# A row-by-row product kernel: four batch rows per instruction, and four 14.6 KB packets where one of 57 KB was stored

## The chip, the cores and the metric

The kernel runs on one core of a Trainium2 chip. The metric is the device time of one execution in microseconds (us). Medians are quoted. In the views of the profile VectorE is DVE, ScalarE is ACT and SyncE, which issues the stores, is SP. A packet, in the profile, is a run of bytes that one of the core's 16 DMA engines moves in one piece; in the stores it is one contiguous run of a partition (before: 9,600 such packets of 4,096 to 58,624 B for 75 stores of 128 partitions).

## The reference

For each of 4,096 batch rows of 256 fp32 numbers, the output holds all products x[i]·x[j] with j ≥ i, one triangle row after the other:

```python
def _L0_rec_ref(inputs):                     # inputs: [4096, 256] float32
    d = inputs.shape[1]
    dot = jnp.einsum('bi,bj->bij', inputs, inputs)
    iu, ju = jnp.triu_indices(d)
    return dot[:, iu, ju]                    # [4096, 32896] float32
```

The input is 4.2 MB and the output 539 MB. The work is one multiplication per number stored.

## The kernel before

A group is 512 batch rows: 128 partitions with four batch rows each. A partition's four output rows lie one behind the other in memory, so they are treated as one run of 131,584 numbers and cut into nine pieces of about 14,600. Each piece has one buffer, filled by multiplications of a single triangle row (`tensor_scalar` on VectorE or `activation` on ScalarE, shared out by estimated time), and is stored by one DMA in which each partition is one contiguous run of 57 KB.

```python
x_in = x.rearrange("(g p r) d -> p g r d", p=P, r=REPEAT)        # REPEAT = 4
x_out = out.rearrange("(g p r) c -> g p (r c)", p=P, r=REPEAT)
xt = xpool.tile([P, groups, REPEAT, d], F32, name="x")
...                                                              # loads cut
for g in range(groups):
    for c, (lo, hi) in enumerate(zip(borders, borders[1:])):     # nine pieces
        o = opool.tile([P, slot], F32, tag="o", name=f"o_{g}_{c}")   # three buffers
        cuts = [lo, *FIRST, hi] if g == c == 0 else [lo, hi]
        for a, b in zip(cuts, cuts[1:]):
            shares.even()
            for row, i, j, at, length in runs(d, a, b):
                shares.multiply(o[:, at - lo : at - lo + length],
                                xt[:, g, row, j : j + length],
                                xt[:, g, row, i : i + 1], length)
            nc.sync.dma_start(x_out[g][:, a:b], o[:, a - lo : b - lo])
```

Of the kernel before, what the change touches and what calls it, by code (L numbers as in the profile page):

```python
# [1 line left out]

# [4 lines left out]

F32 = mybir.dt.float32
AF = mybir.ActivationFunctionType
ALU = mybir.AluOpType  # L10

P = 128
UNIT = 64


def even_borders(lo: int, hi: int, pieces: int) -> list[int]:
    units = (hi - lo) // UNIT
    return [lo + units * c // pieces * UNIT for c in range(pieces)] + [hi]


def runs(d: int, lo: int, hi: int):


    width = d * (d + 1) // 2
    for row in range(lo // width, (hi + width - 1) // width):
        at = row * width
        for i in range(d):
            a, b = max(at, lo), min(at + d - i, hi)
            if a < b:
                yield row, i, i + a - at, a, b - a  # L30
            at += d - i


class Shares:


    def __init__(self, nc):
        self.nc = nc
        self.vector = self.scalar = 0.0

    def even(self):
        self.vector = self.scalar = 0.0

    def multiply(self, dst, src, factor, length: int):
        v = self.vector + 130 + 0.51 * length
        s = self.scalar + 187 + 0.83 * length
        if v <= s:
            self.vector = v
            self.nc.vector.tensor_scalar(dst, src, factor, None, ALU.mult)  # L49
        else:  # L50
            self.scalar = s
            self.nc.scalar.activation(dst, src, AF.Copy, scale=factor)  # L52


REPEAT = 4
PIECES = 9
FIRST = [1024, 3072, 7168]


@with_exitstack  # L60
def kernel(
    ctx: ExitStack, tc: tile.TileContext, x: bass.AP, out: bass.AP
):




    nc = tc.nc
    n, d = x.shape
    width = out.shape[1]  # L70
    assert n % (P * REPEAT) == 0 and width == d * (d + 1) // 2
    groups = n // (P * REPEAT)
    total = REPEAT * width
    assert total % UNIT == 0
    borders = even_borders(0, total, PIECES)
    slot = max(b - a for a, b in zip(borders, borders[1:]))

    xpool = ctx.enter_context(tc.tile_pool(name="x", bufs=1))
    opool = ctx.enter_context(tc.tile_pool(name="o", bufs=3))

    x_in = x.rearrange("(g p r) d -> p g r d", p=P, r=REPEAT)
    x_out = out.rearrange("(g p r) c -> g p (r c)", p=P, r=REPEAT)

    xt = xpool.tile([P, groups, REPEAT, d], F32, name="x")
    cuts = sorted({0, 1, groups // 8, groups // 2, groups})
    for a, b in zip(cuts, cuts[1:]):
        if a < b:
            nc.sync.dma_start(xt[:, a:b], x_in[:, a:b])

    shares = Shares(nc)  # L90
    for g in range(groups):
        for c, (lo, hi) in enumerate(zip(borders, borders[1:])):
            o = opool.tile([P, slot], F32, tag="o", name=f"o_{g}_{c}")
            cuts = [lo, *FIRST, hi] if g == c == 0 else [lo, hi]
            for a, b in zip(cuts, cuts[1:]):
                shares.even()
                for row, i, j, at, length in runs(d, a, b):
                    shares.multiply(
                        o[:, at - lo : at - lo + length],
                        xt[:, g, row, j : j + length],  # L100
                        xt[:, g, row, i : i + 1],
                        length,
                    )
                nc.sync.dma_start(x_out[g][:, a:b], o[:, a - lo : b - lo])  # L104


# [1 line left out]
_INS = ["r_inputs"]  # L108
_OUTS = [((4096, 32896), "float32")]


# [20 lines left out]
```

## Time and profile before

| | before |
|---|---|
| time, median of 3 (range) | 1287.72 us (1287.57 to 1287.92) |
| VectorE busy | 977 us, 4,961 instructions |
| ScalarE busy | 968 us, 3,299 instructions |
| data moved, packets of the data queue | 543.17 MB, 11,872 |
| packets of the instruction queue | 66 |

The first lines to read are the data queue's share (98.0%) and what ended the engines' idle time (stores): both are quoted in the prediction below, with the last windows of the span. One more line completes the picture. It is the chain of work that ended last, followed back from the end and summed by line.

```profile
DMA out_dram<-o 65%; DVE o L49 31%; DMA x<-in_r_inputs_dram 0%; DVEq L49 0%; SPq L104 0%; DVEq L128 0%
```

Two thirds of the chain is storing; VectorE's third are the steps by which a freed buffer is filled again. A buffer comes free when the latest engine is done with it: the last four stores land 0.4 to 0.5 us after every eighth packet of the engine that ends at 1284.6 us, and VectorE goes on 0.12 to 0.13 us after a landing.

### The profile page before, as it was taken

What the parts mean: (1) busy time and instruction counts of PE and PEld (TensorE: products, weight loads), DVE (VectorE), ACT (ScalarE), POOL (GpSimd) and SP (SyncE); (2) the same over time, 40 slices, a digit from 0 to 9 for tenths busy, and PEclk for the clock granted to TensorE, in tenths of its full rate; (3) what the DMA queues carried; (4) which work ended last, traced back from release to release, by engine and by line L of the source; (5) the groups of instructions that cost most, each with busy time, mean ns of one, the idle gap of its engine ahead of it and who ended that gap; (6) DMA issues with size and microseconds to landing.
All of it is one profiled execution on the core that took longest, in us unless ns stands there. A gap on an engine that the chain in (4) does not pass through costs nothing.

```text
span 1285.9 us, 8601 instructions
## 1 busy us (share of the span) xinstructions
DVE 977.2 (76%) x4961; ACT 968.2 (75%) x3299; POOL 0.2 (0%) x4
## 2 busy tenths in 40 slices
DVE  8987778777777777777777777777777777688760
ACT  9987778777777777777777777777777777687760
POOL 0000000000000000000000000000000000000000
DMA  9999999999999999999999999999999999999995
GB/s 392 435 434 435 437 435 427 426 428 437 433 435 436 437 435 433 437 432 428 421 435 437 419 426 435 420 426 412 437 410 437 434 411 412 437 433 435 413 408 222
DMA packets 11938, 543.71 MB, mean 423 GB/s; under 512 B 1248, under 2 KB 1248, under 8 KB 2400
## 3 DMA queue, kind: packets, MB, share of 16 engines
q1 hardware_dynamic: 11872, 543.17, 98.0%
q14 instruction: 66, 0.54, 0.1%
HBM read 4.19 MB, written 538.97 MB: 422 GB/s over the span
## 4 chain that ended last, share of the span: by engine, by line
DMA 66%; DVE 31%; issue 0%; DVEq 0%; SPq 0%
DMA out_dram<-o 65%; DVE o L49 31%; DMA x<-in_r_inputs_dram 0%; DVEq L49 0%; SPq L104 0%; DVEq L128 0%
## 5 line engine op out<-in xcount | busy, mean ns | idle before, releaser
L49 DVE TENSOR_SCALAR o<-x 128x256 f32<-128x256 f32 (+53 forms) x4961 | 977.2, 288 | 274.1 <-DMA out_dram<-o 269.8
L52 ACT ACTIVATE o<-x 128x255 f32<-128x255 f32 (+62 forms) x3298 | 967.0, 387 | 282.2 <-DMA out_dram<-o 280.0
L52 ACT ACT_TABLE_LOAD x1 | 1.3, 1283 | 0.7 <-PEq L119 0.7
L119 POOL MEMSET const-bfloat16-1.0<- 128x1 bf16 x1 | 0.1, 101 | 0.0
L119 POOL MEMSET const-uint8-127<- 128x1 uint8 x1 | 0.1, 101 | 0.0
L119 POOL MEMSET const-float32-0.0<- 128x1 f32 x1 | 0.1, 98 | 0.2 <-issue 0.2
L119 POOL MEMSET const-float32-1.0<- 128x1 f32 x1 | 0.1, 98 | 0.0
## 6 DMA issues: line engine op xcount, KB each, us to landing
out_dram<-o SPq DMA_DIRECT2D x39, 7296.0 KB, 41.9
out_dram<-o SPq DMA_DIRECT2D x32, 7328.0 KB, 35.9
out_dram<-o SPq DMA_DIRECT2D x1, 3712.0 KB, 17.9
x<-in_r_inputs_dram SPq DMA_DIRECT2D x1, 2048.0 KB, 12.5
out_dram<-o SPq DMA_DIRECT2D x1, 2048.0 KB, 14.3
x<-in_r_inputs_dram SPq DMA_DIRECT2D x1, 1536.0 KB, 7.0
out_dram<-o SPq DMA_DIRECT2D x1, 1024.0 KB, 12.1
x<-in_r_inputs_dram SPq DMA_DIRECT2D x1, 512.0 KB, 3.3
```

What stands on the lines that cost most here:

```text
L49: self.nc.vector.tensor_scalar(dst, src, factor, None, ALU.mult)
L52: self.nc.scalar.activation(dst, src, AF.Copy, scale=factor)
L119: nc = _bacc.Bacc("TRN2", target_bir_lowering=False, num_devices=1)
```

## The change

One `tensor_tensor` multiplies the same triangle row, or two neighbouring ones, of all four batch rows. VectorE can do that with access patterns that step from batch row to batch row and repeat the factor (971 such instructions in the changed kernel). ScalarE gets only what VectorE has no time for. The store keeps its number of bytes, but in a buffer [partition, batch row, piece] a partition's share is four runs of 14.6 KB, which go to four output rows. The intent: far fewer instructions, at the price of more and shorter packets.

```diff
-    xt = xpool.tile([P, groups, REPEAT, d], F32, name="x")
+    total = n // P * d
+    xt = xpool.tile([P, total + 1], F32, name="x")      # a product of two rows reads one column more
+    nc.vector.memset(xt[:, total:], 0.0)
...                                                      # rows dealt out anew: "(p g r) c -> g p r c"
-            o = opool.tile([P, slot], F32, tag="o", name=f"o_{g}_{c}")
+            o = opool.tile([P, REPEAT, slot], F32, tag="o", name=f"o_{g}_{c}")
...                                                      # ScalarE's rows, vector_ops, split: cut
+                for way, (i, j, at, length) in interleave(block[k:]):
+                    if way == "each": ...               # four tensor_scalar, as before
+                    m = 2 if way == "two" else 1
+                    nc.vector.tensor_tensor(
+                        o[:, :, at : at + m * length].rearrange("p r (m l) -> p r m l", m=m),
+                        window(xt[:, row + j :], [[d, REPEAT], [1, m], [1, length]]),
+                        window(xt[:, row + i :], [[d, REPEAT], [1, m], [0, length]]),
+                        ALU.mult,
+                    )
-                nc.sync.dma_start(x_out[g][:, a:b], o[:, a - lo : b - lo])
+                nc.sync.dma_start(x_out[g][:, :, a:b], o[:, :, a - lo : b - lo])
```

More of the change, by code (lines that the diff above doesn't have):

```diff
@@ L13 @@
 UNIT = 64
+REPEAT = 4
+PIECES = 9
+BUDGET = 1.08
+FIRST = [512, 1536, 3584]
 def even_borders(lo: int, hi: int, pieces: int) -> list[int]:
@@ L18, in even_borders @@
     return [lo + units * c // pieces * UNIT for c in range(pieces)] + [hi]
-def runs(d: int, lo: int, hi: int):
-    width = d * (d + 1) // 2
-    for row in range(lo // width, (hi + width - 1) // width):
-        at = row * width
-        for i in range(d):
-            a, b = max(at, lo), min(at + d - i, hi)
-            if a < b:
-                yield row, i, i + a - at, a, b - a
-            at += d - i
-class Shares:
-    def __init__(self, nc):
-        self.nc = nc
-        self.vector = self.scalar = 0.0
-    def even(self):
-        self.vector = self.scalar = 0.0
-    def multiply(self, dst, src, factor, length: int):
-        v = self.vector + 130 + 0.51 * length
-        s = self.scalar + 187 + 0.83 * length
-        if v <= s:
-            self.vector = v
-            self.nc.vector.tensor_scalar(dst, src, factor, None, ALU.mult)
-        else:
-            self.scalar = s
-            self.nc.scalar.activation(dst, src, AF.Copy, scale=factor)
@@ L55, with runs, vector_ops @@
-REPEAT = 4
-PIECES = 9
-FIRST = [1024, 3072, 7168]
+def runs(d: int, lo: int, hi: int) -> list:
+    found, at = [], 0
+    for i in range(d):
+        a, b = max(at, lo), min(at + d - i, hi)
+        if a < b:
+            found.append((i, i + a - at, a, b - a))
+        at += d - i
+    return found
+def vector_ops(block: list) -> list:
+    ops, k = [], 0
+    while k < len(block):
+        i, j, at, n = block[k]
+        two = k + 2 < len(block) and i == j
+        each = REPEAT * (130 + 0.52 * n)
+        together = 68 + 1.046 * REPEAT * n - (34 if two else 0)
+        if each <= together:
+            ops.append(("each", block[k]))
+        elif two:
+            ops.append(("two", block[k]))
+            k += 1
+        else:
+            ops.append(("all", block[k]))
+        k += 1
+    return ops
@@ new lines, in interleave, with vector_time @@
+def interleave(block: list) -> list:
+    half, at = 0, sum(n for *_, n in block) / 2
+    while half < len(block) and at > 0:
+        at -= block[half][3]
+        half += 1
+    a, b = vector_ops(block[:half]), vector_ops(block[half:])
+    return [op for k in range(max(len(a), len(b))) for ops in (a, b) for op in ops[k : k + 1]]
+def vector_time(block: list) -> float:
+    t = 0.0
+    for way, (i, j, at, n) in vector_ops(block):
+        if way == "each":
+            t += REPEAT * (130 + 0.52 * n)
+        else:
+            t += 68 + 1.046 * REPEAT * n * (2 if way == "two" else 1)
+    return t
@@ L60, with split, window @@
+def split(block: list, budget: float) -> int:
+    scalar, k = 0.0, 0
+    while k < len(block):
+        scalar += REPEAT * (184 + 0.837 * block[k][3])
+        if vector_time(block[k:]) <= budget or scalar > vector_time(block[k + 1 :]):
+            break
+        k += 1
+    return k
+def window(ap: bass.AP, free: list) -> bass.AP:
+    return bass.AP(ap.tensor, ap.offset, [list(ap.ap[0]), *free])
 @with_exitstack
@@ L70 @@
     width = out.shape[1]
-    assert n % (P * REPEAT) == 0 and width == d * (d + 1) // 2
+    assert n % (P * REPEAT) == 0 and width == d * (d + 1) // 2 and width % UNIT == 0
     groups = n // (P * REPEAT)
-    total = REPEAT * width
-    assert total % UNIT == 0
-    borders = even_borders(0, total, PIECES)
+    borders = even_borders(0, width, PIECES)
     slot = max(b - a for a, b in zip(borders, borders[1:]))
@@ L79 @@
     opool = ctx.enter_context(tc.tile_pool(name="o", bufs=3))
-    x_in = x.rearrange("(g p r) d -> p g r d", p=P, r=REPEAT)
-    x_out = out.rearrange("(g p r) c -> g p (r c)", p=P, r=REPEAT)
-    xt = xpool.tile([P, groups, REPEAT, d], F32, name="x")
-    cuts = sorted({0, 1, groups // 8, groups // 2, groups})
+    x_in = x.rearrange("(p r) d -> p (r d)", p=P)
+    x_out = out.rearrange("(p g r) c -> g p r c", p=P, r=REPEAT)
+    total = n // P * d
+    xt = xpool.tile([P, total + 1], F32, name="x")
@@ L86 @@
+    nc.vector.memset(xt[:, total:], 0.0)
+    cuts = [0, REPEAT * d, total // 2, total]
     for a, b in zip(cuts, cuts[1:]):
-        if a < b:
-            nc.sync.dma_start(xt[:, a:b], x_in[:, a:b])
-    shares = Shares(nc)
+        nc.sync.dma_start(xt[:, a:b], x_in[:, a:b])
     for g in range(groups):
         for c, (lo, hi) in enumerate(zip(borders, borders[1:])):
-            o = opool.tile([P, slot], F32, tag="o", name=f"o_{g}_{c}")
-            cuts = [lo, *FIRST, hi] if g == c == 0 else [lo, hi]
+            o = opool.tile([P, REPEAT, slot], F32, tag="o", name=f"o_{g}_{c}")
+            first = g == c == 0
+            cuts = [lo, *(FIRST if first else []), hi]
@@ L95 @@
             for a, b in zip(cuts, cuts[1:]):
-                shares.even()
-                for row, i, j, at, length in runs(d, a, b):
-                    shares.multiply(
-                        o[:, at - lo : at - lo + length],
-                        xt[:, g, row, j : j + length],
-                        xt[:, g, row, i : i + 1],
-                        length,
+                block = runs(d, a, b)
+                k = split(block, 0.0 if first else BUDGET * REPEAT * (b - a))
+                for i, j, at, length in block[:k]:
+                    for r in range(REPEAT):
+                        row = (g * REPEAT + r) * d
+                        nc.scalar.activation(
+                            o[:, r, at - lo : at - lo + length],
+                            xt[:, row + j : row + j + length],
+                            AF.Copy,
+                            scale=xt[:, row + i : row + i + 1],
+                        )
@@ new lines @@
+                row = g * REPEAT * d
+                for way, (i, j, at, length) in interleave(block[k:]):
+                    at -= lo
+                    if way == "each":
+                        for r in range(REPEAT):
+                            row_r = row + r * d
+                            nc.vector.tensor_scalar(
+                                o[:, r, at : at + length],
+                                xt[:, row_r + j : row_r + j + length],
+                                xt[:, row_r + i : row_r + i + 1],
+                                None,
+                                ALU.mult,
+                            )
+                        continue
+                    m = 2 if way == "two" else 1
[3 more added lines that the diff above has]
+                        window(xt[:, row + i :], [[d, REPEAT], [1, m], [0, length]]),
+                        ALU.mult,
```

## The prediction

> **What bounds the kernel now.** I read the page first: the DMA queues beside the engines' busy shares, then the groups of instructions.
>
> ```profile
> DVE 977.2 (76%) x4961; ACT 968.2 (75%) x3299; POOL 0.2 (0%) x4
> ...
> q1 hardware_dynamic: 11872, 543.17, 98.0%
> q14 instruction: 66, 0.54, 0.1%
> HBM read 4.19 MB, written 538.97 MB: 422 GB/s over the span
> ...
> L49 DVE TENSOR_SCALAR o<-x 128x256 f32<-128x256 f32 (+53 forms) x4961 | 977.2, 288 | 274.1 <-DMA out_dram<-o 269.8
> L52 ACT ACTIVATE o<-x 128x255 f32<-128x255 f32 (+62 forms) x3298 | 967.0, 387 | 282.2 <-DMA out_dram<-o 280.0
> ```
>
> Both engines idle a fifth of the time, and nearly all of that waiting for a stored buffer to come free. The data queue is busy 98.0% of 16 DMA engines' span. So the store is the limit, and faster arithmetic alone buys nothing. What matters is the 2% that is not busy, and who has it. For that I cut the end of the span, after the last compute instruction, into windows of 2 us (columns: window and its length; DVE, ACT and POOL busy; clock; share of 16 DMA engines; GB/s, each packet counted where it starts).
>
> ```profile
> 1264.00:1266.00 2.00, 0.00 (x0) 0.00 (x0) 0.00 (x0) 1.00 1.08 469
> 1266.00:1268.00 2.00, 0.00 (x0) 0.00 (x0) 0.00 (x0) 1.00 1.08 469
> 1268.00:1270.00 2.00, 0.00 (x0) 0.00 (x0) 0.00 (x0) 1.00 0.14 59
> 1270.00:1272.00 2.00, 0.00 (x0) 0.00 (x0) 0.00 (x0) 1.00 0.14 59
> 1272.00:1274.00 2.00, 0.00 (x0) 0.00 (x0) 0.00 (x0) 1.00 0.14 59
> 1274.00:1276.00 2.00, 0.00 (x0) 0.00 (x0) 0.00 (x0) 1.00 0.07 29
> 1276.00:1278.00 2.00, 0.00 (x0) 0.00 (x0) 0.00 (x0) 1.00 0.00 0
> 1278.00:1280.00 2.00, 0.00 (x0) 0.00 (x0) 0.00 (x0) 1.00 0.07 29
> ```
>
> A packet here is one partition's 58,624 B, which in 2 us is 29 GB/s. Until 1268 all 16 engines start a packet per window (469 = 16 x 29). Then 14 of them have finished, two go on, and from 1274 one alone. The end of the kernel is one DMA engine that is 15 us late.
>
> Stringing the trace's single DMA packets (start, duration, size, queue) into 16 lines shows why. Packets follow each other without a gap. Fourteen lines end at 1269.6 us, one at 1275.5, one at 1284.6. From 739 us on each of the fourteen also stood idle for about 12 us in 8 gaps of 1.1 to 2.1 us, when no finished buffer was there, since buffers come free only when the latest engine is done. Without those they would have ended at about 1257.5, so the last engine has **27 us of extra work**. On the two late lines stand instruction-fetch packets of 8,192 B (309 ns), and the data packet beside such a fetch takes about 2.60 us on one of them and 2.35 us on the other instead of 2.15. The program has 5,040 VectorE and 3,378 ScalarE instructions; at 128 per packet that is 39 and 26 fetches. I infer that the last engine carries VectorE's: 27.1 us / 39 = 0.69 us each (309 + 450 ns by the single packets).
>
> [...] The old pitch is 526,336 B; the new is 4,210,688 B, that is 4 MiB + 16 KiB. [...]
>
> **The change, part by part.**
>
> 1. *Fewer instructions.* The built program has 1,892 on VectorE (848 tensor_scalar, 971 tensor_tensor, the rest mostly waits) and 633 on ScalarE. VectorE's fetches shrink in proportion: 27.1 x 1,892 / 5,040 = 10.2 us. On the line that sets the end: **-16.9 us**.
>
> 2. *Shorter packets.* Bytes stay. From start to start the trace's packets take 155.3 ns (4,096 B), 305.8 (8,192), 607 (16,384) and 2,150.6 (58,368): 0.03677 ns per byte plus 4.6 ns. A partition's piece is now four packets, three more. An engine has 8 partitions and 72 pieces: 576 x 3 x 4.6 ns = **+7.9 us**, on every line.
>
> 3. *Start.* The first piece must come from slower arithmetic. With about 130 + 0.52n ns per tensor_scalar (VectorE ran without a stop over the first 174: 34.99 us, 201 ns each at a mean length near 140, so it fits), piece 0 is ready at 4.0 + 11.4 = 15.4 us and piece 1 at about 30.9, near 32 with the issue. The queue has input until about 13 us and then 17.8 us of piece 0, until about 31. **+1 us** of an idle queue on all lines.
>
> 4. *VectorE.* [...] A group of nine pieces then has some 120 tensor_tensor over 98,920 elements, 111 us, and 108 tensor_scalar, 28 us: 139 us against 9 x 17.4 = 157 us of storing. But the built program makes 102 instructions of a group wait for the one directly before them, although the code interleaves two halves to avoid that: a two-row product is taken to overlap everything between its first and last element. Completion trails the next start by 357 - 263 = 94 ns at 256 columns, and from VectorE's last end to the store's issue 60 ns pass, so such a wait should cost some 150 ns: 15 us more, 154 of 157. It stays just hidden. The first two-row product of a piece likewise waits for ScalarE's rows, 8 us in the ninth piece; that lies within the two buffers still queued. **0 us.**
>
> Sum: -16.9 + 7.9 + 1 = -8.0; 1287.7 - 8.0 = 1279.7, or **1279.5 us**.
>
> **The rivals.** *VectorE becomes the bound.* For it: only 3 us of room per group, and the late pieces exceed 17.4 us alone (the ninth: 40 instructions, 38 of which wait, 21 us). If the wait costs 0.18 to 0.23 us, the room is gone; at 0.25, 25.5 us of waiting make a group 164 us, and the whole 8 x 164 + 20 = 1330 us. Against it: the author's pacing constant leaves room, and three buffers even out the pieces. *The store gets slower,* by the pitch: [...] I know nothing that speaks for it. *Nothing is saved at the end,* because fetches aren't the cause of the lateness: then packets alone count, and 1287.7 + 9 = 1297. Against it, two late lines with just the two kinds of long packets. *The start and the packets cost less:* 1272.
>
> **Range and chances.** The steps of the sum are each good to some 4 us, which gives 1272 to 1287; VectorE's waits widen the upper side only. Range 1271 to 1300. Over 2% faster is under 1262, and even without any fetch the packets' own time forbids it: 0.02. Over 2% slower, above 1313, needs a wait of over 0.22 us or a slow pitch: 0.11. Within 2%: 0.87.
>
> **What would show it.** The instruction queue should hold about 20 packets before and in the span in place of 72, the data queue about 40,000, with 98 to 99% of the span. The last windows should show one late engine, by about 10 us less than now. VectorE should be busy 88 to 95%, ScalarE about 11%. Idle VectorE time should still be ended by out-DMAs, and the queue should be empty once, near 31 us. Packets of 14,592 B should take about 541 ns from start to start; longer ones mean the pitch. If VectorE hardly waits for DMA after the first pieces and the queue's share falls under 97%, the first rival has won and the prediction is wrong.

## The result, and the profile after

The changed kernel took **1287.36 us** (1287.25 to 1287.59, 4 runs), the kernel before 1287.66 us in the same rounds. Ratios here are the mean time of one kernel's fast runs over that of the other's of the same rounds, so not quite the ratio of the quoted medians: 0.9998, with a 95% interval of 0.998 to 1.0015. The time did not move; 8 us less were predicted.

The page of the changed kernel, in the lines that answer to those of before:

```profile
DVE 1165.9 (91%) x1820; ACT 161.6 (13%) x561; POOL 0.2 (0%) x4
...
q1 hardware_dynamic: 40032, 543.17, 100.0%
q14 instruction: 21, 0.17, 0.0%
...
DVE o L159 42%; DMA out_dram<-o 32%; DVE o L150 15%; ACT o L138 5%; ACTq L138 0%; ACTq L189 0%; SPq L165 0%; DVEq L159 0%
...
L159 DVE TENSOR_TENSOR o<-x 128x72 f32<-128x72 f32 (+58 forms) x971 | 962.1, 1005 | 88.9 <-ACT o L138 67.2
L138 ACT ACTIVATE o<-x 128x87 f32<-128x87 f32 (+18 forms) x560 | 160.3, 370 | 1077.3 <-DMA out_dram<-o 883.2
```

The instructions are gone as built, and the instruction packets fell from 66 to 21: 45 fewer for 5,893 fewer VectorE and ScalarE instructions in the built programs, 131 to a packet where the prediction counts 128. The data queue went from 98.0% to 100.0% of the span without moving a byte more: its packets take longer (net of gaps 1279.7 us against 1259.0, in the table below). The chain now names VectorE most often, which looks like a new bound, but the line of VectorE has only 88.9 us of idle time, ended by ScalarE, whose own idle time is ended by stores. Page and chain leave open who limits whom; experiment 5 decides it.

The last windows of the changed kernel (columns as in the prediction):

```profile
1278.00:1280.00 2.00, 0.00 (x0) 0.00 (x0) 0.00 (x0) 1.00 0.94 401
1280.00:1282.00 2.00, 0.00 (x0) 0.00 (x0) 0.00 (x0) 1.00 0.13 52
1282.00:1284.00 2.00, 0.00 (x0) 0.00 (x0) 0.00 (x0) 1.00 0.07 30
```

The tail of one late engine has shrunk from 15 us to about 4, but the fourteen undisturbed engines now end at 1280 where they ended at 1269.6. The gain at the tail has been lost in the body.

Where it was lost shows only when single packets are read, as in the prediction. In the body I read, for each kernel, when the fourteen undisturbed engines end, how long the queue was empty on them before that (gaps in which at most three of the 16 engines worked, from 15 us on), how much later the last engine ends, and the mean recorded time of a packet of 14,592 B. "Net" is the end without the gaps. The table includes the experiments that follow, since all of them are read the same way (times in us, packets in ns):

```
kernel       14 end  empty   net   last later  14,592 B   row starts in the buffer, modulo 256 B
before       1269.7  10.7  1259.0   14.9        -         (57 KB packets)
few57        1257.2   0.0  1257.2    0.8        -         (57 KB packets)
few_split    1268.9   0.0  1268.9    0.6       546.8      128 and 0 in turn
split_wide   1274.8   0.0  1274.8    0.4       550.5      always 128
few14        1278.0   0.0  1278.0    0.6       550.8      always 160
after        1280.5   0.8  1279.7    3.9       551.5      always 160
after32w     1270.4   0.9  1269.5    4.4       547.2      0 and 128 in turn
after32      1269.4   4.5  1264.9    4.9       545.2      always 0
```

The last column is from the built programs' allocation, not from the trace: the first output buffer starts at byte 49,280 of each partition in the kernel before and at 49,312 in the changed one, rows follow each other at the buffer's stride.

### The profile page after: what moved, and what is told of

It is laid out like the page before. It is cut to its first block, busy times and chain, and to the rows that moved or that the text cites. A ratio compares the mean times of both kernels' runs of the same rounds, so it can differ in the third digit from the quotient of the medians.

```text
span 1285.6 us, 2706 instructions
## 1 busy us (share of the span) xinstructions
DVE 1165.9 (91%) x1820; ACT 161.6 (13%) x561; POOL 0.2 (0%) x4
## 4 chain that ended last, share of the span: by engine, by line
DVE 57%; DMA 32%; ACT 5%; issue 2%; ACTq 0%; SPq 0%; DVEq 0%
DVE o L159 42%; DMA out_dram<-o 32%; DVE o L150 15%; ACT o L138 5%; ACTq L138 0%; ACTq L189 0%; SPq L165 0%; DVEq L159 0%
## 5 line engine op out<-in xcount | busy, mean ns | idle before, releaser
L159 DVE TENSOR_TENSOR o<-x 128x72 f32<-128x72 f32 (+58 forms) x971 | 962.1, 1005 | 88.9 <-ACT o L138 67.2
L138 ACT ACTIVATE o<-x 128x87 f32<-128x87 f32 (+18 forms) x560 | 160.3, 370 | 1077.3 <-DMA out_dram<-o 883.2
L150 DVE TENSOR_SCALAR o<-x 128x237 f32<-128x237 f32 (+26 forms) x848 | 229.0, 337 | 3.5 <-DMA x<-in_r_inputs_dram 3.5
```

The lines of the kernel that those rows point to most:

```text
L138: nc.scalar.activation(o[:, r, at - lo : at - lo + length], xt[:, row + j : row + j + length], AF.Copy, scale=xt[:, row + i : row + i + 1],)
L150: nc.vector.tensor_scalar(o[:, r, at : at + length], xt[:, row_r + j : row_r + j + length], xt[:, row_r + i : row_r + i + 1], None, ALU.mult,)
L159: nc.vector.tensor_tensor(o[:, :, at : at + m * length].rearrange("p r (m l) -> p r m l", m=m), window(xt[:, row + j :], [[d, REPEAT], [1, ...
```

## The experiments

18 kernels were run, each beside runs of the kernel before on the same chip (1287.7 to 1287.8 us each time). All whose names begin with few, split_first and split_wide give a wrong result: they keep the stores and replace nearly all arithmetic.

### 1. few57: what do the fetches cost the kernel before?

The stores of the kernel before, each piece filled by four wide multiplications on VectorE: 367 VectorE instructions in the built program instead of 5,040 (the 379 in the expectation is the count of few14's program).

```diff
-                for row, i, j, at, length in runs(d, a, b):
-                    shares.multiply(...)
...                                                      # flat: the input tile as one row per partition
+                for at in range(a - lo, b - lo, 4096):
+                    length = min(4096, b - lo - at)
+                    nc.vector.tensor_scalar(o[:, at : at + length], flat[:, :length], flat[:, :1], None, ALU.mult)
```

> The kernel before with its stores, buffers and packets of 57 KB as they are, but four wide multiplications per piece in place of some 110 narrow ones (wrong result on purpose): 379 VectorE and 8 ScalarE instructions. If instruction fetches make the last DMA engine 27 us late, they nearly vanish (3 left, 2 us) and all engines end near 1258 to 1260 us: 1261 to 1264 us. If the lateness has another cause (an engine that is slow by itself), about 1287 us.

Measured: **1261.04 us** (ratio 0.9793, 0.9778 to 0.9807). Its page:

```profile
DVE 591.9 (47%) x289; POOL 0.2 (0%) x4
...
q1 hardware_dynamic: 11872, 543.17, 99.8%
q14 instruction: 4, 0.03, 0.0%
```

The same packets, and 26.7 us less. The prediction had put the last engine's extra work at 27.1 us from the traces.

### 2. few57i: is it the instructions, or the arithmetic?

few57 with 64 one-column multiplications more per piece: nearly as many VectorE instructions as the kernel before (4,907), few products more, ScalarE nearly unused.

```diff
+                if b == hi:
+                    for k in range(64):
+                        nc.vector.tensor_scalar(o[:, 8192 + k : 8193 + k], flat[:, k : k + 1], flat[:, :1], None, ALU.mult)
```

> The stores-only kernel with 57 KB packets (1261.0 us), plus 64 multiplications of a single column per piece on VectorE (same values again, wrong result on purpose): 4,907 VectorE instructions, ScalarE still 8. If fetching VectorE's program delays one DMA engine by 0.69 us per 128 instructions, one engine is some 26 us late: 1285 to 1289 us, with hardly any arithmetic added. If the lateness of the kernel before came from the traffic of its arithmetic, or from ScalarE: 1261 to 1265 us.

Measured: **1295.97 us** (ratio 1.0065, 1.005 to 1.008), 34.9 us over few57 and 7 us beyond the expectation. Its windows, from the start of the kernel and from the end (columns: window, length; DVE and POOL busy; clock; DMA share; GB/s):

```profile
22.00:24.00 2.00, 2.00 (x17) 0.00 (x0) 1.00 0.03 12
...
38.00:40.00 2.00, 2.00 (x16) 0.00 (x0) 1.00 0.00 0
...
1272.00:1274.00 2.00, 0.00 (x0) 0.00 (x0) 1.00 0.95 410
1274.00:1276.00 2.00, 0.00 (x0) 0.00 (x0) 1.00 0.27 117
...
1278.00:1280.00 2.00, 0.00 (x0) 0.00 (x0) 1.00 0.07 29
...
1290.00:1292.00 2.00, 0.00 (x0) 0.00 (x0) 1.00 0.07 29
```

The first two lines are a flaw of the experiment. The 64 instructions also delay the first pieces, and the queue stood empty for 2.7 us from 22 us on and for 7.0 us from 34 us on (single packets). The rest of the 34.9 us is 25.2 us, for 35 instruction packets more than few57 (39 against 4): 0.72 us each. The last lines show one engine alone for about 15 us, 29 GB/s being one packet per window. VectorE is busy for 1,149 us of this kernel, more than in the kernel before, but it does not pace it, since it still waits for stores:

```profile
DVE o L100 <- DMA out_dram<-o: 101.0, 61, 2.3
```

(Engine and line, what it waited for, us in total, times, longest.) So instructions alone make an engine late.

### 3. few14, few_split, split4 and few_split8: what do shorter packets cost?

few14 is the changed kernel's stores with four wide multiplications per piece. few_split is few57 with the destination unchanged, and only the buffer cut into four rows with a gap after each, which makes four packets. split4 is the whole kernel before with those gaps (right result). few_split8 has eight packets.

```diff
 # few14, against the changed kernel
-                block = runs(d, a, b)
...
+                for r in range(REPEAT):
+                    nc.vector.tensor_scalar(o[:, r, a - lo : b - lo], xt[:, : b - a], xt[:, :1], None, ALU.mult)
 # few_split and split4, against few57 and the kernel before (few_split8: 8 and slot // 8 + 8)
-            o = opool.tile([P, slot], F32, tag="o", name=f"o_{g}_{c}")
+            o = opool.tile([P, 4, slot // 4 + 16], F32, tag="o", name=f"o_{g}_{c}")
...
+                nc.sync.dma_start(x_out[g][:, a:b].rearrange("p (k w) -> p k w", w=part), o[:, k:e, :part])
```

> The changed kernel with its stores as they are (packets of 14.6 KB, same layout) and four wide multiplications per piece (wrong result on purpose). No empty queue near 32 us is expected, as pieces are ready early. Theory P, the short packet itself costs 11 ns and not 4.6: packets keep a mean near 551 ns, about 1281 us. Theory S, packets are slowed because all engines start in step after the empty queue, or by VectorE's arithmetic: they fall to 545 ns and the time to about 1268 us.

> The kernel before, with each partition's 57 KB cut into four packets of 14.6 KB by gaps in the buffer; the destination stays contiguous, arithmetic and layout stay, 213 instructions more (1.5 us). Theory P (11 ns for each of 1,728 more packets per engine, and some 70 ns on all engines at each of 72 issues): 1308 to 1312 us. By the prediction's 4.6 ns per packet: 1297 us. If the packet size does not matter and the row pitch of the changed kernel was the cause: under 1291 us.

> Stores only (wrong result on purpose): the layout of the kernel before, 72 issues, each partition's 57 KB cut into four packets of 14.6 KB by gaps in the buffer, the destination contiguous. If every shorter packet costs about 12 ns, as between the two stores-only kernels, 1279 to 1283 us. If it costs the 4.6 ns of the prediction and the rest comes from the jump to another row after each packet: 1268 to 1271 us.

> The same with eight packets of 7.3 KB: 2,304 more packets per engine than with four, the same 72 issues. At 4.6 ns each 10.6 us more than with four; at 9 ns (4.6 plus some 4.5 of late packets) 21 us more; at 12 ns 28 us more.

Measured: few14 **1281.80 us** (ratio 0.9954), split4 **1299.40** (1.009), few_split **1272.82** (0.9884), few_split8 **1298.94** (1.0088). Against few57, few14 is 20.8 us longer, which is 12 ns for each of 576 × 3 = 1,728 more packets per engine, and not the predicted 4.6 ns. But few_split, with packets of nearly the same lengths, is only 11.8 us longer (6.8 ns), and split4 likewise 11.6 us over the kernel before, between the two figures of its expectation. So the price is not one of length alone: **9.0 us** stand between few_split and few14. A further halving costs more than in proportion (26.1 us, 11.3 ns per packet), but there the rows' stride of 7,360 B also puts three of four starts off a 256 B boundary, which experiment 7 will show to matter.

The page's GB/s in 40 slices of 32 us shows that the price is not constant either. Here is few14:

```profile
GB/s 379 431 430 430 426 427 427 424 426 429 426 424 425 427 426 426 425 426 425 427 425 427 425 426 425 428 426 426 426 426 426 426 426 425 427 425 427 425 426 396
```

After the first slice it moves 430 GB/s for three slices, from the fifth on mostly 426. By single packets, one of 14,592 B takes 545.0 ns on average from 30 to 100 us and 551.4 ns after 140 us. In the changed kernel itself they take 551 to 552 ns from 30 us on. The prediction's 4.6 ns rested on the short packets of the kernel before, all of the first 32 us.

### 4. pitch, few14u, few14x2, few14c: four candidates for the 9.0 us

pitch is the changed kernel with the row assignment of before (526,336 B between partitions; right result). few14u is few14 with all cuts of a row at multiples of 512 B. few14x2 is few14 with two issues per piece. few14c is few14 with its four packets written one behind the other, not into four output rows; what its expectation does not say, its rows in the buffer are also 64 B longer (14,912 B).

```diff
 # pitch, against the changed kernel
-    x_out = out.rearrange("(p g r) c -> g p r c", p=P, r=REPEAT)
+    x_out = out.rearrange("(g p r) c -> g p r c", p=P, r=REPEAT)
...                                                      # the loads to match
 # few14u, against few14
-UNIT = 64
+UNIT = 128
...                                                      # one first piece fewer
 # few14x2, against few14
+                for r in (0, 2):
+                    nc.sync.dma_start(x_out[g][:, r : r + 2, a:b], o[:, r : r + 2, a - lo : b - lo])
 # few14c, against few14
-            o = opool.tile([P, REPEAT, slot], F32, tag="o", name=f"o_{g}_{c}")
+            o = opool.tile([P, REPEAT, slot + 16], F32, tag="o", name=f"o_{g}_{c}")
...
+                nc.sync.dma_start(x_out[g][:, REPEAT * a : REPEAT * b].rearrange("p (k w) -> p k w", w=b - a), o[:, :, a - lo : b - lo])
```

> The changed kernel with the old assignment of rows to partitions (a pitch of 526,336 B instead of 4,210,688 B between partitions), all else the same. If the pitch slows the packets: 545 ns and 1273 to 1279 us. If not (theories P and S): within 2 us of the changed kernel, 1285 to 1289 us.

> Stores only, packets of 14.6 KB in the changed kernel's layout (1281.8 us), but pieces cut at multiples of 512 B in place of 256 B (packets of 14,336 and 14,848 B). If packets that start at an odd 256 B cause the part beyond the 4.6 ns: 1270 to 1276 us. If not: 1281 to 1283 us.

> Stores only, packets of 14.6 KB in the layout of the changed kernel, but every piece's store as two issues of two rows each, so 150 issues in place of 75 with the same packets. If the 70 ns by which all engines are late at each issue is a cost per issue: 1281.8 plus 5 = 1286 to 1288 us. If it goes by the packets issued: 1281 to 1283 us.

> few14 unchanged in its loads, first pieces, packet sizes and assignment of rows, but the four packets of a partition are written one behind the other into the output, and not each into another output row (wrong result on purpose). It parts the two terms in the 20.8 us that the short packets cost. If the jump to another row after every packet costs the 9.0 us by which few14 stands over few_split: 1272 to 1274 us, as few_split (1272.8). If the 9.0 us come from what else differs between those two (the input's layout, the pieces at the start, 4 MiB between partitions): 1281 to 1282, as few14.

Measured: pitch **1287.01 us** (ratio 0.9994), few14u **1281.44**, few14x2 **1282.52**, few14c **1281.59**. All four candidates fall: none moves the time by more than 0.7 us. (The 70 ns per issue of two expectations are near what the changed kernel's trace has: after 61 of its last 70 store issues, 1.3 to 2.6 us later, 13 to 16 packets take 50 to 73 ns more than the median of 549. Twice the issues cost few14x2 only the 0.7 us.) Before few14c ran I had taken the jump to another output row for the cause; that theory fell with it.

### 5. nowait: is VectorE the bound?

Only the way in which the output of a two-row product is written down differs, so that the program no longer makes it wait for its predecessor and for ScalarE (right result).

```diff
-                        o[:, :, at : at + m * length].rearrange("p r (m l) -> p r m l", m=m),
+                        o[:, :, at : at + m * length],
```

> The changed kernel, with the output of a two-row product written as one run, so that the program no longer makes it wait for the instruction before it and for ScalarE's rows that it does not touch. Theory: the store is the bound, VectorE ends earlier or waits for buffers, the time stays at 1286 to 1288 us. Rival (VectorE paces the kernel, its chain being 57% of the last chain): 3 to 15 us faster, 1272 to 1284 us.

Measured: **1287.52 us** (ratio 0.9998, 0.9983 to 1.0013). Its waits (engine and line, what it waited for, us in total, times, longest):

```profile
DVE o L159 <- DMA out_dram<-o: 102.0, 49, 3.2
```

The chain that ended last, of its page:

```profile
DMA out_dram<-o 59%; DVE o L159 34%; DVE o L150 3%; DMA x<-in_r_inputs_dram 0%; DVEq L159 0%; SPq L165 0%
```

VectorE ran faster (its `tensor_tensor` are busy for 911.1 us in place of 962.1) and spent what it gained waiting for stores; the chain now names the store first, at the same time of the whole. In the changed kernel the store is the bound, and the chain's 42% for VectorE is work that would otherwise have waited.

### 6. split_first, few14f, few14p, split_wide: what else differs?

split_first is few_split with the small first pieces of the changed kernel, and few14f is few14c with the first piece stored as in few_split. few14p is few14c with the loads and row assignment of before. Both keep few14c's longer rows. split_wide is few_split with rows of 14,848 B in the buffer, not 14,720.

```diff
 # split_first, against few_split
+            cuts = [0, 512, 1536, 3584, part] if g == c == 0 else [0, part]
 # few14f, against few14c
+                for k, e in ((0, 1), (1, 2), (2, 3), (3, 4)) if first else ((0, 4),):   # store rows k to e
 # few14p, against few14c
-    x_in = x.rearrange("(p r) d -> p (r d)", p=P)
+    x_in = x.rearrange("(g p r) d -> p g r d", p=P, r=REPEAT)
 # split_wide, against few_split
-            o = opool.tile([P, 4, slot // 4 + 16], F32, tag="o", name=f"o_{g}_{c}")
+            o = opool.tile([P, 4, 3712], F32, tag="o", name=f"o_{g}_{c}")
```

> few_split with the small first pieces that the changed kernel has (512, 1024, 2048 and 64 columns of four rows), all else as few_split. If the start decides in which state the queue then runs: 1281 to 1282. If not: 1272.8 to 1273.5. Wrong result on purpose.

> few14c with the first piece stored as few_split stores it, row by row, one packet of 14.6 KB per partition and issue. If the start decides: 1272 to 1274. If not: 1281 to 1282. Wrong result on purpose.

> few14c with the loads and the assignment of rows to partitions of the kernel before. If these, and not the start, hold the 9.0 us: 1272 to 1274. If not: 1281 to 1282. Wrong result on purpose.

> few_split with rows of 14,848 B in the buffer, as few14 has them, in place of 14,720 B. If the stride of the buffer holds the 9.0 us: 1281 to 1282. If not: 1272.8 to 1273. Wrong result on purpose.

Measured: split_first **1273.24 us**, few14f **1281.26**, few14p **1281.71**: three more candidates gone. split_wide: **1278.47 us**, 5.6 us over few_split. Only the place of the rows in the buffer differs between these two, so the place has a price. (Some packets of both start off a 256 B boundary in the output too, but the same ones in both.)

### 7. after32 and after32w: the address of the buffers

The changed kernel's input tile has one column of 4 B more than it had. That moves all output buffers from 49,280 B, which is 128 B beyond a multiple of 256, to 49,312 B, 160 B beyond. after32 has 32 spare columns in place of 1, which puts the buffers at 49,408 = 193 × 256. after32w also gives the buffer's rows a stride of 14,976 B = 58.5 × 256. Both results are right.

```diff
-    xt = xpool.tile([P, total + 1], F32, name="x")
+    xt = xpool.tile([P, total + 32], F32, name="x")
 # after32w, besides
-            o = opool.tile([P, REPEAT, slot], F32, tag="o", name=f"o_{g}_{c}")
+            o = opool.tile([P, REPEAT, slot + 32], F32, tag="o", name=f"o_{g}_{c}")
```

> The changed kernel with 32 spare columns after the input instead of 1, so that the output buffers start at 49,408 B (a multiple of 128) and not at 49,312 B (32 B off a multiple of 64); nothing else. If the buffers' address is the rest of the 9.0 us: about 1284 us. If not: 1287.2 to 1287.6. Right result.

> after32 with rows of 14,976 B (117 x 128) in the buffer in place of 14,848 (116 x 128, 29 x 512). If address and stride are the 9.0 us: 1278 to 1279 us. If the stride alone: 1281.5 to 1282. If neither works here: 1287.2 to 1287.6. Right result.

Measured: after32 **1277.14 us** (ratio to before 0.9917, 0.9903 to 0.993), after32w **1277.72 us** (0.9922, 0.991 to 0.9935). The address alone brings 10.2 us (besides it only one `memset` of the start is wider), more than either theory had. The one column is hardly to blame for it, though: by the allocation, without it the rows would start 128 B beyond, as in split_wide, whose packets cost nearly as much (550.5 ns). What gains the time is that the 32 columns put them on a boundary. The changed kernel without any spare column, and the kernel before with aligned buffers, were not run. The page of after32:

```profile
GB/s 366 425 432 432 428 432 431 432 432 427 433 432 432 432 428 433 432 432 430 428 428 432 431 432 416 432 432 431 432 416 430 430 430 432 415 432 432 432 430 347
...
q1 hardware_dynamic: 40032, 543.17, 99.7%
q14 instruction: 21, 0.17, 0.0%
...
L159 DVE TENSOR_TENSOR o<-x 128x72 f32<-128x72 f32 (+58 forms) x971 | 962.5, 1006 | 79.1 <-ACT o L138 57.4
```

The packets and instructions are those of the changed kernel; the queue now keeps 428 to 432 GB/s in most slices to the end. By single packets, 98.7% of those of 14,592 B take exactly 545 ns, and the mean is 545.2 against 551.5 ns. The three slices at 415 and 416 GB/s hold new gaps: the queue was empty for 1.1 to 1.3 us at 779, 937 and 1,094 us. The store has become so fast that the arithmetic is at the edge of not keeping up. That explains why a net gain of 14.8 us (1279.7 − 1264.9 in the table) gives 10.2: 3.7 us went into gaps, and the last engine is 1 us later.

I had expected after32w to be the better of the two, for a stride like few_split's. It is not, and the table's last column orders its six kernels with packets of this size in one way: row starts always on a multiple of 256 B, 545.2 ns; every second one, 546.8 and 547.2; always 128 B beyond, 550.5; always 160 B beyond, 550.8 and 551.5. The other eight kernels with such packets fit: 546.6 and 546.7 where every second row starts on a multiple (split_first, split4), 550.8 to 551.5 where none does (pitch, nowait, few14x2, few14c, few14f, few14p).

Why this is so stays open. By the means, 160 B beyond cost 6.3 ns (between after32 and after) and 128 B 5.3 (between after32 and split_wide). The single packets of other runs do not fit a fixed price for an offset (after 150 us, strung into 16 lines; I take every four in a line for the four rows of a partition). In few_split and after32w aligned and unaligned packets alternate, and the median is 545 ns for both: an unaligned start alone costs a packet nothing there, and the higher mean comes mostly from the 3 to 4% of packets that take over 560 ns. In few14c the four rows start 160, 224, 32 and 96 B beyond a multiple; its packets of at most 560 ns take 550.1, 550.2, 548.2 and 548.8 ns on average, against 545.1 in after32, so 32 B cost 3 ns and 224 B only 5.

So what the runs show is that the place of the rows has a price and that starts on multiples of 256 B avoid it; they do not show what sets its size, nor why few14's packets paid nothing at first (545.0 ns from 30 to 100 us, 551.4 after 140 us).

### 8. pair2: a version that beats both

Two batch rows at a time, five pieces, packets of 26 KB, and only two-row products written as in nowait (right result).

```diff
-REPEAT = 4
-PIECES = 9
-BUDGET = 1.08
-FIRST = [512, 1536, 3584]
+REPEAT = 2
+PIECES = 5
+BUDGET = 0.95
+FIRST = [1024, 3072]
...
-        if each <= together:
+        if n < 2:
```

> A version made from both findings, correct: two batch rows at a time in place of four, so that packets have 26 KB (1,280 per engine in place of 2,304), only two-row products on VectorE with exact outputs (1,912 instructions), ScalarE taking more (1,667). From 1261.0 for bare stores: 704 more packets than with 57 KB at some 10 ns, 7 us; 13 to 15 fetches on VectorE's DMA engine at 0.66 us, partly covered, 5 to 9 us: 1273 to 1278 us. If VectorE or ScalarE paced it: over 1290 us.

Measured: **1274.28 us** (ratio 0.9897, 0.9881 to 0.9914), 1.0% below both kernels. VectorE and ScalarE in its page:

```profile
L157 DVE TENSOR_TENSOR o<-x 128x484 f32<-128x484 f32 (+59 forms) x1793 | 1014.5, 635 | 222.5 <-DMA out_dram<-o 210.0
L136 ACT ACTIVATE o<-x 128x256 f32<-128x256 f32 (+48 forms) x1580 | 494.6, 403 | 740.5 <-DMA out_dram<-o 726.2
```

Here VectorE again waits for stores (210 us of its idle time), so there is room. Which of its changes brings the gain was not parted. (Its expectation took 0.66 us for a fetch and 10 ns for a shorter packet; few57i shows 0.72 us, few_split and few14 6.8 and 12 ns.) Its buffers start at 49,312 B too; an aligned pair2 was not run.

## Why the prediction was wrong

**What bounds the kernel** was right. Removing nearly all instructions and no packet gave 26.7 us for a reading of 27.1. After the change the store is still the bound (nowait).

**Step 1, fewer instructions (−16.9 us).** The cause was right, the size too small. It assumed that the remaining 10.2 us shrink in proportion. Measured, the last engine is 3.9 us late in the changed kernel and 4.9 us in after32. In after32 fifteen of the 21 instruction packets stand beside a data packet of 815 to 900 ns instead of 545, and 15 times about 350 ns is 5.2 us. (The prediction's cost of a fetch does not add up: 309 + 450 ns are 0.76 us, not 0.69; few57i has 0.72.) Why the fetch's own 309 ns do not add here, while few57i shows 0.72 us per fetch with 57 KB packets, no run tells. With −26.7 for all fetches and about 4 to 5 us for the remainder, this step is worth about −22.

**Step 2, shorter packets (+7.9 us).** This is the step that failed. Net of gaps the packets of the changed kernel cost 1279.7 − 1257.2 = 22.5 us over those of few57 (13 ns for each of 1,728 more packets per engine), not 7.9. The prediction read 4.6 ns per packet and took it to hold for every packet of the kernel. With aligned buffers it nearly does: after32's net end is 7.7 us over few57's (4.5 ns for each packet more; few57's own packets all start 128 B off, which may cost it something). The missing term is the address: every row of every buffer starts 160 B beyond a 256 B boundary, and 14.8 us net (10.2 us of time) hang on that. The prediction did not ask where the packets start. The rival "the store gets slower" came true in kind but named the wrong reason: the pitch of 4 MiB + 16 KiB, for which no trace spoke, changes nothing (pitch, with 526,336 B: 1287.01 us). So the sign misled too, "about 541 ns from start to start; longer ones mean the pitch": the median is 541 in after32 and 546 in the changed kernel, with the same pitch.

**Step 3, the start (+1 us)** was right. These two windows of the changed kernel show the queue running dry while VectorE works on:

```profile
30.00:32.00 2.00, 2.00 (x6) 0.00 (x0) 0.00 (x0) 1.00 0.53 164
32.00:34.00 2.00, 1.97 (x2) 1.75 (x7) 0.00 (x0) 1.00 1.11 467
```

By single packets the queue is empty for 0.8 us at 31.3 us; each engine is idle for about 1.1.

**Step 4, VectorE stays hidden (0 us)** was right in the changed kernel, for a store that was slower than foretold. The arithmetic was sized well: nowait, nearly without waits for the instruction before, has VectorE busy for 140.5 us per group (1,124.0 us in all), for 139 foretold. The prediction's 111 us for the `tensor_tensor` of a group was the estimate. The trace of the changed kernel has 70 + 1.043 ns per element from start to start (168 that overlapped the next one, 72 to 1,768 elements), which makes 111.7 us for a group. For `tensor_scalar` the trace of before has 129 + 0.521 ns per element (4,895 of them), for 130 + 0.52 in the prediction. With the store at the predicted speed it is off by little: the three gaps of after32, 3.5 us together. Of the signs that were to show it, VectorE's 91% was right and "idle time ended by out-DMAs" was wrong: ScalarE waited for the buffers and passed the wait on. The prediction's own test for the first rival had two halves. One came true, VectorE hardly waiting for DMA; the other, a queue share under 97%, did not (100.0%), and nowait decides against the rival.

The sum in steps that were each measured: 1287.7 (before) − 26.7 (all fetches: few57) + 11.8 (four packets for one: few_split, half of whose rows are off the boundary) + 9.0 (what few14 has over few_split: 5.6 for the place of the rows, split_wide, and 3.4 that were not parted) + 5.6 (what instructions and start remain: after − few14) = 1287.4. The aligned version, 1277.1 us, is 2.4 us below the prediction, its errors in steps 1 and 4 partly cancelling. That the changed kernel's own time still lies between 1271 and 1300 us is luck: step 1 erred by about 5 us in the other direction, and the range went beyond 1287 only for VectorE's waits, which did not make the kernel longer.

## What to carry to other kernels

Where the store is the bound, count what else travels on the DMA engines: here the fetches of 5,000 instructions cost 26.7 us through one late engine, and here thinning them out was worth more than a faster VectorE (nowait: 51 us less of `tensor_tensor`, 1287.52 us in place of 1287.36). When packets get shorter, look at the address at which each starts: 31 more spare columns in another tile moved all buffers onto a boundary and saved 10.2 us, and no line of the profile names it. Read the cost of a packet from the whole span, not from its first windows: few14's took 545.0 ns from 30 to 100 us and 551.4 after 140.
